# Layer norm's Newton step on VectorE, a local branch stored as half-rows, and a new order of steps

## The chip, the core and the metric

The program runs on one core of a Trainium2 chip. The metric is the device time of one execution in microseconds (us), the median of three. A core has five engines, each with its own instruction queue, worked off in order: TensorE (PE; its weight loads are shown apart as PEld), VectorE (DVE), ScalarE (ACT), GpSimd (POOL) and SyncE (SP), which here only issues DMAs. SBUF is the working memory. PSUM is the small memory that TensorE writes its results to; VectorE and ScalarE can use it too. An engine that needs another's result waits on a semaphore, and everything behind the waiting instruction in its queue waits with it.

## The reference, cut to what matters

Two layers on x of shape (32, 128, 56, 56), all in fp32. Layer 0 (a depthwise convolution, a layer norm, and a mixture of 8 experts of which each token uses 2) is not touched. Layer 1 is:

```
xh  = cv1_w @ x + cv1_b                        # 128 channels, per pixel
l   = silu(batchnorm(depthwise_conv3x3(xh)))   # the local branch
t   = (xh - mean) / sqrt(var + 1e-05)          # over the channels of a pixel
x,z = in_proj(t); x = silu(conv1d(x)); dt, B, C = x_proj(x); dt = softplus(dt_proj(dt))
h_i = exp(dt * A_i) * h_i + dt * B_i * x       # along the 3136 pixels, 16 states i, 256 channels
g   = out_proj((sum_i C_i * h_i + D * x) * silu(z))
out = x + cv2_w @ concat(l, g) + cv2_b
```

## The kernel before

Layer 1 (`layer1`, from L960) works through 224 groups, seven of 448 pixels in each of the 32 images. The 256 inner channels lie as two halves on 128 partitions, so most tiles are 128 x 896. A group has 16 units, one per state i (the recurrence of `h_i`). Each unit is a chain over the engines:

- `bc_load` (SP, L1320): a row of B (`bb`) or C (`cb`) for two states, broadcast to 128 partitions by one DMA, three buffers each
- `db_pool` (POOL, L1326): db = du * bb
- `exp_act` (ACT, L1339): da = exp(dt * A_i), two instructions, into a PSUM tile; `das` holds two such tiles, used by even and odd units in turn. A tile is 1024 columns wide, of which columns 63 to 960 are used
- `scan_dve` (DVE, L1357 and L1361): the recurrence over the 448 pixels. `MODE` gives each state a letter: in mode D the result overwrites da, in modes P and Q it goes to a tile `hs` in SBUF, in Q as two halves
- `cmul` (L1377): prod = h * cb, on VectorE for D, on GpSimd for P and Q; six buffers `prod`
- `carry_act` (ACT, L1383 and L1385): the last column of h into db, for the next group
- `sum_pe` (PE, L1286): adds the product into the PSUM tile `py`

Beside the units each group has the steps of `PLAN`: `fetch` (DMAs of x and of layer 0's result), `moe_pe`/`moe_act`, `cv1_pe` (xh, and again with centred weights for the variance), `sq_act`, `var_pe` (L1065: the variance of 4 x 112 pixels as a 112 x 4 tile), `rstd_act` and `rstd_dve` (1/sqrt of it), `bc_pe` (that, broadcast to all partitions), `te_dve` (the normalized input, L1106), `z_pe` and `xm_pe` (in_proj with the 1-D convolution folded in), the silus, `px_pe`/`px_act` (dt, B, C, and out to DRAM), `dt_pe` with `sp_abs`, `sp_exp`, `sp_one`, `sp_w`, `sp_ln`, `sp_pe`, `sp_act` (softplus), `du_pool` (L1241), `lt_pe`, `lt_act`, `lt_silu` (the local branch), and at the end `yz_dve`, `out_pe`, `out_act`. All TensorE results but `py` and the two `da` share two PSUM buffers (`mm_tile`).

The order is written out. Every entry of `PLAN` and `UNITS` has a key in units; at the end of `layer1` all steps of all groups are sorted by 16 x group + key (units: 16 x group + i + key) and emitted so. Each engine's queue is that list cut to its own steps. The steps of a group thus run from about three groups ahead of its units to two behind, and a key that changes moves the step in its engine's queue.

`rstd_act` and `rstd_dve` compute r = 1/sqrt(var + eps) as exp(-0.5 * ln(.)), refined by one Newton step, all on ScalarE: `v` = -0.5 * (var + eps) (L1072), Ln (L1074), Exp (L1075), Square (L1083), then, column by column with per-partition scales, four instructions for w * v + 1.5 (L1089) and four for the last product (L1091). `lt_act` turns the two PSUM tiles of the local branch, each holding a half of the rows on each partition half, into one tile of 128 channels x 448 pixels with four instructions of 64 partitions (L1267). `out_pe` then sums four things into `p_out`: x by the identity (L1302), the local branch by `cvlt` (L1303), and two halves of the state branch (L1306). In fp32 each matmul is recorded as two passes.

Of the kernel before, what the change touches and what calls it, by code (L numbers as in the profile page):

```python
# [13 lines left out]
C = 128  # L14
# [31 lines left out]
    (-49.034, "fetch"),  # L46
    (-34.491, "moe_pe"),
    (-33.235, "moe_act"),
    (-30.254, "cv1_pe", "p_cvc", "cv1c"),
    (-25.768, "sq_act"),  # L50
    (-25.59, "cv1_pe", "p_cv1", "cv1t"),
    (-25.289, "var_pe"),
    (-25.26, "cv1_act"),
    (-23.34, "rstd_act"),
    (-21.787, "rstd_dve", 0),
    (-21.347, "edges_act"),
    (-20.085, "rstd_dve", 1),
    (-19.667, "rstd_dve", 2),
    (-19.068, "bc_pe"),
    (-18.585, "te_dve"),  # L60
    (-17.079, "z_pe", 0),
    (-16.851, "z_copy", 0),
    (-16.382, "te_act"),
    (-16.257, "z_pe", 1),
    (-15.595, "xm_pe", 0),
    (-15.307, "xm_pe", 1),
    (-15.128, "z_copy", 1),
    (-14.156, "xm_act", 0),
    (-14.083, "z_silu"),
    (-13.778, "xm_act", 1),  # L70
    (-13.661, "px_pe"),
    (-13.36, "tables"),
    (-11.232, "px_act"),
    (-10.854, "dt_pe", 0),
    (-9.505, "dt_pe", 1),
    (-9.422, "sp_abs", 0),
    (-8.888, "sp_abs", 1),
    (-8.888, "sp_exp"),
    (-7.793, "sp_one"),
    (-6.852, "sp_w"),  # L80
    (-5.494, "sp_pe", ("w", "e", "m")),
    (-5.47, "sp_ln"),
    (-5.277, "sp_pe", ("u",)),
    (-4.8, "sp_act", 0),
    (-4.714, "sp_act", 1),
    (-4.647, "du_pool"),
    (-4.258, "lt_pe", range(0, 9)),
    (-3.101, "lt_act", 0),
    (-3.069, "lt_act", 1),
    (1.649, "lt_silu"),  # L90
    (2.601, "dd_pe"),
    (18.368, "yz_dve", 0),
    (18.991, "yz_dve", 1),
    (22.686, "out_pe"),
    (25.881, "out_act"),
# [3 lines left out]
        (-5.616, "bc_load", "cb"),  # L99
        (-4.911, "bc_load", "bb"),  # L100
        (-1.39, "exp_act"),
        (-1.071, "db_pool"),
        (-0.072, "scan_dve"),
        (0.16, "cmul", 0),
        (1.101, "carry_act"),
        (3.822, "sum_pe"),
    ),
    (
        (-2.061, "db_pool"),
        (-0.79, "exp_act"),  # L110
        (0.509, "scan_dve"),
        (1.024, "cmul", 0),
        (1.612, "carry_act"),
        (9.256, "sum_pe"),
    ),
    (
        (-6.765, "bc_load", "bb"),
        (-2.879, "db_pool"),
        (-0.932, "bc_load", "cb"),
        (-0.582, "exp_act"),  # L120
        (0.048, "scan_dve"),
        (0.16, "cmul", 0),
        (0.522, "carry_act"),
        (5.894, "sum_pe"),
    ),
    (
        (-3.304, "db_pool"),
        (-1.398, "exp_act"),
        (-0.808, "scan_dve"),
        (0.16, "cmul", 0),  # L130
        (0.573, "carry_act"),
        (1.195, "sum_pe"),
    ),
    (
        (-8.644, "bc_load", "bb"),
        (-3.115, "db_pool"),
        (-1.883, "bc_load", "cb"),
        (-1.034, "exp_act"),
        (0.401, "scan_dve"),
        (1.06, "cmul", 0),  # L140
        (1.952, "carry_act"),
        (2.601, "sum_pe"),
    ),
    (
        (-4.077, "db_pool"),
        (-0.798, "exp_act"),
        (-0.026, "scan_dve"),
        (0.16, "cmul", 0),
        (1.627, "carry_act"),
        (4.902, "sum_pe"),  # L150
    ),
    (
        (-4.927, "bc_load", "bb"),
        (-4.793, "db_pool"),
        (-2.544, "bc_load", "cb"),
        (0.282, "exp_act"),
        (0.775, "scan_dve"),
        (0.822, "cmul", 0),
        (2.269, "carry_act"),
        (2.348, "sum_pe"),  # L160
    ),
    (
        (-4.809, "db_pool"),
        (-0.316, "exp_act"),
        (-0.083, "scan_dve"),
        (1.06, "cmul", 0),
        (4.835, "sum_pe"),
        (7.392, "carry_act"),
    ),
    (  # L170
        (-5.33, "bc_load", "bb"),
        (-4.423, "db_pool"),
        (-4.3, "bc_load", "cb"),
        (-1.21, "exp_act"),
        (-0.684, "scan_dve"),
        (0.16, "cmul", 0),
        (0.81, "carry_act"),
        (0.846, "sum_pe"),
    ),
    (  # L180
        (-4.428, "db_pool"),
        (-0.91, "exp_act"),
        (-0.218, "scan_dve"),
        (0.16, "cmul", 0),
        (0.687, "carry_act"),
        (2.437, "sum_pe"),
    ),
    (
        (-6.827, "bc_load", "bb"),
        (-5.444, "bc_load", "cb"),  # L190
        (-4.717, "db_pool"),
        (-1.047, "exp_act"),
        (-0.085, "scan_dve"),
        (0.16, "cmul", 0),
        (0.563, "carry_act"),
        (1.1, "sum_pe"),
    ),
    (
        (-5.564, "db_pool"),
        (-0.852, "exp_act"),  # L200
        (0.057, "scan_dve"),
        (0.16, "cmul", 0),
        (0.848, "sum_pe"),
        (1.13, "carry_act"),
    ),
    (
        (-8.236, "bc_load", "bb"),
        (-5.146, "db_pool"),
        (-4.78, "bc_load", "cb"),
        (-0.969, "exp_act"),  # L210
        (0.064, "scan_dve"),
        (1.06, "cmul", 0),
        (3.979, "sum_pe"),
        (4.341, "carry_act"),
    ),
    (
        (-5.525, "db_pool"),
        (-0.5, "exp_act"),
        (-0.221, "scan_dve"),
        (0.16, "cmul", 0),  # L220
        (0.243, "carry_act"),
        (0.9, "sum_pe"),
    ),
    (
        (-12.437, "bc_load", "bb"),
        (-3.699, "db_pool"),
        (-2.866, "bc_load", "cb"),
        (-1.274, "exp_act"),
        (-0.7, "scan_dve"),
        (-0.009, "carry_act"),  # L230
        (0.16, "cmul", 0),
        (0.341, "sum_pe"),
    ),
    (
        (-4.484, "db_pool"),
        (-1.264, "exp_act"),
        (-0.768, "scan_dve"),
        (1.211, "cmul", 0),
        (2.733, "sum_pe"),
        (5.051, "carry_act"),  # L240
# [4 lines left out]
def tile_kernel(tc: tile.TileContext, a: dict, out: bass.AP):  # L245
# [14 lines left out]
    with (  # L260
# [414 lines left out]
        def weights(wp, wt, pw):  # L675
# [24 lines left out]
            cvlt = load(a["cv2_wT"][:C, :], [C, C], "cvlt")  # L700
# [259 lines left out]
def layer1(s):  # L960
# [12 lines left out]
    with (  # L973
# [12 lines left out]
        das = [pda.tile([128, 1024], F32, name=f"da{i}")[:, 512 - W1 : 512 + W1] for i in range(2)]  # L986
# [7 lines left out]
        one5 = one.tile([128, 1], F32, name="one5")  # L994
        nc.vector.memset(one5, 1.5)
        eps5h = one.tile([128, 1], F32, name="eps5h")
        nc.vector.memset(eps5h, -0.5e-5)
# [71 lines left out]
        def rstd_act(g):  # L1069
            d = st[g]  # L1070
            d["v"] = two.tile([TT, TPC1], F32, name="v")
            nc.scalar.activation(d["v"], d.pop("p_var")[:TT, :TPC1], AF.Identity, bias=eps5h[:TT], scale=-0.5)  # L1072
            d["r"] = two.tile([TT, TPC1], F32, name="r")
            nc.scalar.activation(d["r"], d["v"], AF.Ln, scale=-2.0)  # L1074
            nc.scalar.activation(d["r"], d["r"], AF.Exp, scale=-0.5)  # L1075

        def rstd_dve(g, k):

            d = st[g]
            r, v = d["r"], d["v"]  # L1080
            if k == 0:
                d["rw"] = two.tile([TT, TPC1], F32, name="rw")
                nc.scalar.activation(d["rw"], r, AF.Square)  # L1083
            else:
                w = d["rw"]
                for j in range(TPC1):
                    c = slice(j, j + 1)
                    if k == 1:
                        nc.scalar.activation(w[:, c], w[:, c], AF.Identity, bias=one5[:TT], scale=v[:, c])  # L1089
                    else:  # L1090
                        nc.scalar.activation(r[:, c], w[:, c], AF.Copy, scale=r[:, c])  # L1091
# [89 lines left out]
        def px_act(g):  # L1181
            d = st[g]
            xd = d["xd"] = two.tile([XR, CH1], F32, name="xd")
            nc.scalar.copy(xd, d.pop("p_x")[:XR, :CH1])
            bc_d = d["bc_d"] = s["dram2"].tile([XR, CH1], F32, name="bc_d")
            nc.sync.dma_start(out=bc_d[DR:, :], in_=xd[DR:, :])
# [72 lines left out]
        def lt_act(g, r):  # L1259
            d = st[g]  # L1260
            if r == 0:
                d["lt"] = two.tile([C, CH1], F32, name="lt")
            lt, p = d["lt"], d["p_l"][r]
            rs = slice(r * HD, (r + 1) * HD)
            for k in range(2):
                ks = slice(k * HD, (k + 1) * HD)
                nc.scalar.activation(  # L1267
                    lt[rs, k * CH1 // 2 : (k + 1) * CH1 // 2], p[ks, : CH1 // 2], AF.Identity,
                    bias=s["bnt"][ks, r, 0:1], scale=s["bnt"][ks, r, 1:2],
                )  # L1270
# [28 lines left out]
        def out_pe(g):  # L1299
            d = st[g]  # L1300
            d["p_out"] = p = mm_tile("p_out")
            nc.tensor.matmul(p[:, :CH1], lhsT=ident, rhs=d.pop("x1"), start=True, stop=False)  # L1302
            nc.tensor.matmul(p[:, :CH1], lhsT=s["cvlt"], rhs=d.pop("lt"), start=False, stop=False)  # L1303
            yz = d.pop("yz")
            for r in range(2):
                nc.tensor.matmul(p[:, :CH1], lhsT=s["wo"][:, r, :], rhs=yz[:, r, :], start=False, stop=r == 1)  # L1306

        def out_act(g):
            n, q = divmod(g, NQ1)
            ot = two.tile([C, CH1], F32, name="ot")  # L1310
# [131 lines left out]
```

## Time and profile before

| | |
|---|---|
| median of three executions | 16079.44 us (16073.9 to 16081.61) |
| the profiled execution | 16086.15 us |
| its span, first to last instruction | 16084.4 us |
| first and last `te` (L1106), 224 in all | 5914.4 and 15980.9 us |
| L1339 ACT exp, 7168 of 128 x 449 | 637 ns each |
| L1267 ACT lt, 896 of 64 x 224 | 516 to 535 ns each |
| L1089 and L1091 ACT, 896 each of 112 x 1 | 0.382 and 0.292 us each, overlapping |
| L1072, L1074, L1075 ACT, 112 x 4 | 262, 206 and 206 ns |

The page is one execution as the hardware profiler took it. Times in it are us from the span's start unless marked ns. A line of a timeline has start, duration (of merged instructions together), engine, line, operation, output<-inputs, shapes, number; in brackets the idle time of the engine just before and what ended it. A line of the waits has who waited at which line for whom, total us, times, longest. "PEclk" is the clock that TensorE was granted, as a share of full speed. "Idle" of VectorE between neighbours can be below zero: instructions of one engine overlap by some 0.08 us.

### The profile page before, as it was taken

How to read it: one execution, taken by the hardware profiler on the slowest of the kernel's cores; microseconds unless marked ns; L12 is line 12 of the kernel's file. 1: busy time of each engine (PE TensorE's matmuls, PEld its weight loads, DVE VectorE, ACT ScalarE, POOL GpSimd, SP SyncE). 2: the span in 40 equal slices, each digit the busy share in tenths (PEclk: the TensorE clock that was granted, in tenths of full speed). 3: DMA queues.
4: the chain of work that ended last, by engine and by line, in shares of the span. 5: the costliest groups of instructions: out<-in, count | busy, mean ns of one | idle time of the engine just before them, and what ended most of it. 6: DMA issues, size and time to landing. Idle time of an engine off the chain costs nothing. (4 is left out here: it accounts for less than half of the span.)

```text
span 16084.4 us, 247325 instructions
## 1 busy us (share of the span) xinstructions
PE 13000.1 (81%) x91637; PEld 7138.1 (44%) x91637; DVE 11071.4 (69%) x10582; ACT 11045.9 (69%) x23222; POOL 13580.1 (84%) x8121
## 2 busy tenths in 40 slices
PE   7996100001999989999999999999999999999998
PEld 6996100000777754444444444444444444444443
DVE  2655400000111139999999999999999999999999
ACT  4655200000444459999999999999999999999998
POOL 2443477777888879999999999999999999999999
PEclk9997555555999999999999999999999999999999
DMA  8785433332555545555555555555555555555555
GB/s 265 228 238 185 176 94 93 97 93 68 71 72 71 70 84 178 182 182 181 178 182 181 179 179 179 179 182 181 179 180 181 180 179 179 178 181 182 180 179 166
DMA packets 1239131, 2572.16 MB, mean 160 GB/s; under 512 B 139336, under 2 KB 676640, under 8 KB 1230240
## 3 DMA queue, kind: packets, MB, share of 16 engines
q1 hardware_dynamic: 1041440, 2361.89, 46.6%
q0 software_dynamic: 196480, 194.45, 7.0%
q8 instruction: 721, 11.81, 0.3%
q14 instruction: 490, 4.01, 0.1%
HBM read 2180.38 MB, written 375.43 MB: 159 GB/s over the span
## 5 line engine op out<-in xcount | busy, mean ns | idle before, releaser
L1326 POOL TENSOR_TENSOR db<-du,bb 128x896 f32<-128x896 f32 x3584 | 6835.8, 1936 | 24.8 <-DMA bb<-bc_d 21.8
L1339 ACT ACTIVATE da<-dt,aneg 128x449 f32<-128x449 f32 x7168 | 4534.9, 637 | 454.4 <-DVE prod L1377 297.4
L1357 DVE TENSOR_TENSOR_SCAN da<-da,db 128x898 f32<-128x898 f32 x2240 | 4525.4, 2020 | 157.9 <-ACT da L1339 157.2
L1286 PE MATMUL py<-prod,ident 64*64 64x448 f32 x28672 | 3279.1, 562 | 158.5 <-DVE prod L1377 150.9
L1377 POOL TENSOR_TENSOR prod<-hs,cb 128x896 f32<-128x896 f32 x1344 | 2603.9, 1937 | 153.8 <-issue 104.7
L1377 DVE TENSOR_TENSOR prod<-da,cb 128x896 f32<-128x896 f32 x2240 | 2439.3, 1089 | 233.2 <-PE py L1286 67.2
L944 ACT COPY xc<-ept 128x512 f32<-128x512 f32 (+1 forms) x248 | 143.9, 580 | 2916.5 <-PE ept L942 2614.5
L850 POOL DMA_INDIRECT buf_d<-xg,slot x1568 | 1641.9, 1047 | 538.4 <-issue 528.5
L902 POOL DMA_INDIRECT res_d<-ys,xb x984 | 1593.9, 1620 | 350.2 <-issue 287.3
L942 PE MATMUL ept<-ident,xb 128*128 128x128 f32 (+1 forms) x984 | 189.0, 274 | 2027.0 <-DMA xb<-buf_d 2023.2
L1286 PEld LDWEIGHTS py<-prod,ident 64*64 64x64 f32 x28672 | 1041.8, 134 | 1687.3 <-issue 969.6
L1357 DVE TENSOR_TENSOR_SCAN hs<-da,db 128x898 f32<-128x898 f32 x896 | 1785.6, 2014 | 0.1
L1122 PE MATMUL p_xm<-te,wk 128*128 128x448 f32 x3584 | 1416.0, 546 | 0.0
L894 DVE TENSOR_TENSOR ys<-py,b2t 128x512 f32<-128x512 f32 (+2 forms) x256 | 170.8, 670 | 1712.2 <-PE py L888 1541.6
L847 DVE COPY xg<-gate 128x28 f32<-128x28 f32 x56 | 12.7, 232 | 1896.2 <-DMA buf_d<-xg,slot 1896.2
L942 PEld LDWEIGHTS ept<-ident,xb 128*128 128x128 f32 (+1 forms) x984 | 124.6, 143 | 2030.7 <-issue 2026.3
L888 PEld LDWEIGHTS py<-w2t,hh 128*128 128x128 f32 x7872 | 938.8, 192 | 187.2 <-issue 113.1
L888 PE MATMUL py<-w2t,hh 128*128 128x128 f32 x7872 | 988.0, 279 | 11.0 <-ACT hh L884 10.7
L1122 PEld LDWEIGHTS p_xm<-te,wk 128*128 128x128 f32 x3584 | 657.5, 189 | 731.7 <-issue 567.3
L379 PE MATMUL pc<-xc,toep 112*112 112x112 f32 (+1 forms) x8192 | 937.4, 270 | 40.5 <-ACT toep L368 37.1
L1361 DVE TENSOR_TENSOR_SCAN hs<-da,db 128x449 f32<-128x449 f32 x896 | 924.9, 1074 | 1.3 <-ACT da L1339 0.9
L379 PEld LDWEIGHTS pc<-xc,toep 112*112 112x112 f32 x8192 | 880.7, 184 | 50.8 <-ACT toep L368 45.1
(238 smaller groups left out, 20802.2 us busy)
## 6 DMA issues: line engine op xcount, KB each, us to landing
cb<-bc_d SPq DMA_DIRECT2D x1792, 448.0 KB
bb<-bc_d SPq DMA_DIRECT2D x1792, 448.0 KB
toep<-toep_d SPq DMA_DIRECT2D x448, 392.0 KB
xg<-res_d SPq DMA_DIRECT2D x56, 1792.0 KB
buf_d<-zero SPq DMA_DIRECT2D x28, 2275.0 KB
xb<-buf_d SPq DMA_DIRECT2D x240, 260.0 KB
xt<-in_x SPq DMA_DIRECT2D x32, 1568.0 KB
res_d<-xa SPq DMA_DIRECT2D x128, 392.0 KB
```

The lines of the kernel that those rows point to most:

```text
L379: nc.tensor.matmul(pc[:, c, :, lo:hi], lhsT=tp[c // 2][:, c % 2, 6 - 2 * o : 8 - 2 * o, :], rhs=s4[:, c, :, lo + o - 1 : hi + o - 1], star ...
L850: apart(nc.gpsimd.indirect_dma_start(out=buf_d[:, :], out_offset=bass.IndirectOffsetOnAxis(ap=slots[k][:, o + j : o + j + 1], axis=0), in_ ...
L888: nc.tensor.matmul(py[:n, j, :], lhsT=hh[:, k, j * 128 : j * 128 + n], rhs=w2t[:, k, :], start=k == 0, stop=k == KF - 1,)
L902: apart(nc.gpsimd.indirect_dma_start(out=res_d[:, :], out_offset=bass.IndirectOffsetOnAxis(ap=xb[:n, j, C + 1 : C + 2].bitcast(I32), axis= ...
L942: nc.tensor.transpose(pt[:, j * 128 : j * 128 + n], xb[:n, j, :C], ident[:n, :n])
L1122: nc.tensor.matmul(p[:, :CH1], lhsT=s["wk"][:, k, hs], rhs=d["te"][:, k : k + CH1], start=k == 0, stop=k == DC - 1 and not first,)
L1286: nc.tensor.matmul(ps[r][h * HD : (h + 1) * HD, :CH1], lhsT=lhsT(rs, h), rhs=rhs[rs, h, :], start=start, stop=stop,)
L1326: nc.gpsimd.tensor_tensor(dbv[i][:, :, 1:], st[g]["du"], units[u].pop("bb"), ALU.mult)
L1339: e = nc.scalar.activation(da[:, h * W1 : (h + 1) * W1], st[g]["dt"][:, h, :], AF.Exp, scale=s["aneg"][:, h, i : i + 1])
L1357: nc.vector.tensor_tensor_scan(hs, da, dbs[i], 0.0, ALU.mult, ALU.add)
L1361: half(u, h, nc.vector.tensor_tensor_scan(hs2[h][:, hh], da[:, hh], dbs[i][:, hh], 0.0, ALU.mult, ALU.add))
L1377: eng.tensor_tensor(w["prod"], w["hs"][0][:, :, 1:], w["cb"], ALU.mult)
```

## The change

1. **Newton step.** `rstd_act` now issues four ScalarE instructions: Ln of the variance, var + eps, and the Exp twice, once into SBUF (`r0`) and once into four unused columns of the first `da` tile in PSUM (`aside`). `rstd_dve` is three VectorE instructions on 112 x 4 elements, each with `aside` as one operand.
2. **Local branch.** `lt` is kept as it lies in PSUM, 128 partitions x 2 x 224: two half-rows per channel. `lt_act` is two instructions of 128 partitions. `cvlt` becomes four 128 x 128 weights, each with zeros for the partitions that belong to the other half of the rows, and `out_pe` uses four matmuls of 224 columns for what was one of 448.
3. **Buffers.** `xd` and `ot` have one buffer instead of two; two constant columns go.
4. **Places.** All keys of `PLAN` and `UNITS` are new. The queues keep most of their order. VectorE's differs only by the three new steps, after the scan of state 11 (two of them) and after the scan of state 12 (one). On ScalarE `lt_silu` comes after the other silus instead of first, `edges_act` stands before the exp of state 10 instead of before that of 12, `lt_act`'s two instructions stand apart, and some carries move. On TensorE `px_pe` comes ahead of `cv1_pe` (`p_cvc`), the two `xm_pe` ahead of the sum of state 12; `sum_pe(3)` lies between the two `dt_pe`; `sum_pe(2)` moves ahead of `out_pe` and `var_pe`; the sums after `var_pe` are those of states 5, 8, 6, 1, 9 instead of 2, 6, 8, 5, 1. On GpSimd the db of state 7 moves ahead of the product of state 1 and that of 11 behind the product of 6. On SP `fetch` comes about half as far ahead, and some loads change places.

The diff, with the keys cut to those of the steps named:

```diff
-    (-25.289, "var_pe"),
-    (-23.34, "rstd_act"),
-    (-21.787, "rstd_dve", 0),
-    (-21.347, "edges_act"),
-    (-20.085, "rstd_dve", 1),
-    (-19.667, "rstd_dve", 2),
+    (-23.306, "var_pe"),
+    (-23.291, "rstd_act"),
+    (-23.185, "edges_act"),
+    (-20.935, "rstd_dve", 0),
+    (-20.876, "rstd_dve", 1),
+    (-19.458, "rstd_dve", 2),
...
-            cvlt = load(a["cv2_wT"][:C, :], [C, C], "cvlt")
+            cvlt = wp.tile([128, 2, 2, C], F32, name="cvlt")
+            nc.gpsimd.memset(cvlt, 0.0)
+            for k in range(2):
+                nc.sync.dma_start(
+                    out=cvlt[k * HD : (k + 1) * HD, k], in_=a["cv2_wT"][:C, :].rearrange("(r d) c -> d r c", r=2)
+                )
...
-        das = [pda.tile([128, 1024], F32, name=f"da{i}")[:, 512 - W1 : 512 + W1] for i in range(2)]
+        das = [pda.tile([128, 1024], F32, name=f"da{i}") for i in range(2)]
+        aside = das[0][:TT, :TPC1]
+        das = [t[:, 512 - W1 : 512 + W1] for t in das]
...
         def rstd_act(g):
             d = st[g]
-            d["v"] = two.tile([TT, TPC1], F32, name="v")
-            nc.scalar.activation(d["v"], d.pop("p_var")[:TT, :TPC1], AF.Identity, bias=eps5h[:TT], scale=-0.5)
-            d["r"] = two.tile([TT, TPC1], F32, name="r")
-            nc.scalar.activation(d["r"], d["v"], AF.Ln, scale=-2.0)
-            nc.scalar.activation(d["r"], d["r"], AF.Exp, scale=-0.5)
+            p = d.pop("p_var")[:TT, :TPC1]
+            rl, d["v"], d["r0"] = (two.tile([TT, TPC1], F32, name=n) for n in ("rl", "v", "r0"))
+            nc.scalar.activation(rl, p, AF.Ln, bias=eps5[:TT])
+            nc.scalar.activation(d["v"], p, AF.Identity, bias=eps5[:TT])
+            nc.scalar.activation(aside, rl, AF.Exp, scale=-0.5)
+            nc.scalar.activation(d["r0"], rl, AF.Exp, scale=-0.5)
 
         def rstd_dve(g, k):
 
             d = st[g]
-            r, v = d["r"], d["v"]
             if k == 0:
-                d["rw"] = two.tile([TT, TPC1], F32, name="rw")
-                nc.scalar.activation(d["rw"], r, AF.Square)
+                nc.vector.scalar_tensor_tensor(aside, aside, -0.5, d["r0"], ALU.mult, ALU.mult)
+            elif k == 1:
+                nc.vector.tensor_tensor(aside, aside, d.pop("v"), ALU.mult)
             else:
-                w = d["rw"]
-                for j in range(TPC1):
-                    c = slice(j, j + 1)
-                    if k == 1:
-                        nc.scalar.activation(w[:, c], w[:, c], AF.Identity, bias=one5[:TT], scale=v[:, c])
-                    else:
-                        nc.scalar.activation(r[:, c], w[:, c], AF.Copy, scale=r[:, c])
+                d["r"] = two.tile([TT, TPC1], F32, name="r")
+                nc.vector.scalar_tensor_tensor(d["r"], aside, 1.5, d.pop("r0"), ALU.add, ALU.mult)
...
-                d["lt"] = two.tile([C, CH1], F32, name="lt")
-            lt, p = d["lt"], d["p_l"][r]
-            rs = slice(r * HD, (r + 1) * HD)
-            for k in range(2):
-                ks = slice(k * HD, (k + 1) * HD)
-                nc.scalar.activation(
-                    lt[rs, k * CH1 // 2 : (k + 1) * CH1 // 2], p[ks, : CH1 // 2], AF.Identity,
-                    bias=s["bnt"][ks, r, 0:1], scale=s["bnt"][ks, r, 1:2],
-                )
+                d["lt"] = two.tile([128, 2, CH1 // 2], F32, name="lt")
+            nc.scalar.activation(
+                d["lt"][:, r, :], d["p_l"][r][:, : CH1 // 2], AF.Identity,
+                bias=s["bnt"][:, r, 0:1], scale=s["bnt"][:, r, 1:2],
+            )
...
             nc.tensor.matmul(p[:, :CH1], lhsT=ident, rhs=d.pop("x1"), start=True, stop=False)
-            nc.tensor.matmul(p[:, :CH1], lhsT=s["cvlt"], rhs=d.pop("lt"), start=False, stop=False)
+            lt = d.pop("lt")
+            for k in range(2):
+                for r in range(2):
+                    nc.tensor.matmul(
+                        p[:, k * CH1 // 2 : (k + 1) * CH1 // 2], lhsT=s["cvlt"][:, k, r, :], rhs=lt[:, r, :],
+                        start=False, stop=False,
+                    )
```

## Prediction

> **What bounds the kernel now.** I read the page's busy shares first. No engine stands alone over the whole run:
>
> ```profile
> PE 13000.1 (81%) x91637; PEld 7138.1 (44%) x91637; DVE 11071.4 (69%) x10582; ACT 11045.9 (69%) x23222; POOL 13580.1 (84%) x8121
> ```
>
> The change touches only layer 1, from about 5900 us on, so next the busy time by stretch (columns: PE, PEld, DVE, ACT, POOL busy, then granted clock, DMA share, GB/s):
>
> ```profile
> 8000.00:9000.00 1000.00, 953.21 (x6757) 434.06 (x6757) 961.61 (x687) 914.73 (x1986) 965.24 (x517) 0.96 0.56 181
> ```
>
> Four engines are 91 to 97% busy; ACT, the engine that the change relieves, is the least busy. What counts is where VectorE waits, since its scans carry the recurrence and every loop of waits runs through it. The waits of VectorE, over the span:
>
> ```profile
> DVE da L1357 <- ACT da L1339: 157.2, 273, 1.0
> DVE prod L1377 <- PE py L1286: 67.2, 56, 1.2
> ```
>
> 273 waits for an exp, 56 for TensorE. The timelines put each at one place. From `te` (L1106) to `te` 222 groups take 45.19 us on average. 168 without a VectorE stall on TensorE take mostly 44.86; 54 take 46.3. In the common kind VectorE stands at one scan, that of state 13:
>
> ```profile
> 8921.76 2.02 DVE L1357 TENSOR_TENSOR_SCAN hs<-da,db 128x898 f32<-128x898 f32 x1
> 8924.47 2.04 DVE L1357 TENSOR_TENSOR_SCAN da<-da,db 128x898 f32<-128x898 f32 x1 [0.69 <-ACT da L1339]
> ```
>
> ScalarE at that moment:
>
> ```profile
> 8919.07 1.31 ACT L1339 ACTIVATE da<-dt,aneg 128x449 f32<-128x449 f32 x2
> 8920.33 0.95 ACT L1236 COPY dt<-p_sp 128x448 f32<-128x448 f32 x2
> 8921.17 1.22 ACT L1089 ACTIVATE rw<-rw,one,v 112x1 f32<-112x1 f32 x4
> 8922.29 0.15 ACT L1385 COPY db<-da 128x2 f32<-128x2 f32 x1
> 8922.33 0.86 ACT L1091 ACTIVATE r<-rw,r 112x1 f32<-112x1 f32 x4
> 8923.08 2.53 ACT L1339 ACTIVATE da<-dt,aneg 128x449 f32<-128x449 f32 x4
> ```
>
> The reader is to see that the Newton step (L1089, L1091) stands in ScalarE's queue between the exps of states 12 and 13, and that the scan's 0.69 us is its lateness.
>
> The 46.3 us groups are another matter. Their granted clock:
>
> ```profile
> 10080.00:10081.00 1.00, 0.29 (x1) 1.00 1.03 416
> 10081.00:10082.00 1.00, 1.00 (x6) 0.69 0.92 355
> 10082.00:10083.00 1.00, 1.00 (x8) 0.50 0.74 272
> ...
> 10087.00:10088.00 1.00, 1.00 (x2) 0.50 0.00 0
> 10088.00:10089.00 1.00, 1.00 (x5) 0.90 0.00 0
> ```
>
> TensorE runs at half clock for 6.8 us, just after the thin `p_dt` matmuls (8 rows) and a wait for ScalarE. In half-us stretches the half-clock spells last 3.41 or 6.83 us, in 186 of the 222 groups: 132 short, 54 long. They begin 20.6 to 22.9 us after `te`, at multiples of 3.413 us. I work with a rule read off these phases: a 3.41 us window with less than about 1.47 us of full-height matmul work makes the next one half-speed. A short spell loses 1.7 us of TensorE and stalls nobody; a long one loses 3.4 and stalls VectorE 1.46.
>
> **The change, part by part.** The sum is for the profiled run (span 16084.4, with 1.75 us around it 16086.15), which is 6.7 above the median of 16079.44; the difference is then put on the median.
>
> *The Newton step leaves ScalarE.* Gone from between the exps of 12 and 13: 1.22 + 0.86 us, and the Square (0.19) ahead. The scan of state 13 then waits for nothing known: exp 12 starts when the product of state 10 is done, and exp 13 needs the product of 11, finished 1.9 us before scan 12 is; an exp pair takes 1.25. I take the whole 157 us; at worst, where something else is late there, none.
>
> *It arrives on VectorE* as three 112x4 instructions after scan 11 and scan 12. Nearest rows:
>
> ```profile
> L403 DVE SCALAR_TENSOR_TENSOR nm<-mv,rs 112x7 f32<-112x7 f32 x128 | 120.6, 951 | 2.0
> L584 DVE SCALAR_TENSOR_TENSOR cand<-step,cand 128x4 f32<-128x4 f32 x48 | 7.8, 162 | 5.1 <-ACT sign L552 0.5
> ...
> L583 DVE TENSOR_SCALAR step<-p_tot 128x4 f32<-128x4 f32 x48 | 7.5, 157 | 0.5 <-PE p_tot L568 0.5
> ```
>
> L403 reads two SBUF operands while GpSimd computes: 143 to 2050 ns. With GpSimd idle (L584) 162, with a PSUM operand (L583) 157. The new ones have one operand in PSUM and run beside GpSimd, like `prod<-da,cb`, which takes 1074 to 1094 ns there throughout. So 0.157 each. VectorE's neighbours overlap by 0.08 when independent and gap 0.11 when one needs the other; the three fill the gap between scan 11 and its product and open one between themselves: 3 x 0.157 - 0.25 = 0.22 us a group, 49 us in 224. Bounds: 0, and 3 x (0.157 + 0.11) = 0.80 us, 179.
>
> *Waits added.* The operand shares PSUM tile da[0] with the even exps, so the accesses must be ordered. ScalarE writes it after product 8, which exp 10 waits for anyway; behind it stand `edges` and exp 10. The first VectorE step must follow exp 12 (over 0.4 us before scan 11 ends); behind it stands product 11. Exp 14 must follow the third, which ends 0.08 us after scan 12; behind exp 14 stands `lt_act`, and scan 14 needs it 3 us later. I take 0; the worst, 0.4 a group. The Trainium skill, "PSUM — Partial Sum Buffer", section "PSUM bank collisions raise a hardware error", speaks against the placing: two engines in one bank and quadrant at the same time are an error, whatever the columns. No run here shows a collision; by that rule the order above is a must, and the sum is the same while those margins hold.
>
> *`lt_act`*: four of 529 ns (L1267) become two, -1.06 us of ScalarE, in a place where ScalarE waits 1.26 us for VectorE next: 0. The four `rstd_act` instructions stand for three, 0.2 us each: 0.
>
> *The padded weights.* The `lt` part of `p_out` (L1303) takes 0.75 us unthrottled (8908.37 to 8909.12: two passes of 0.375). It becomes eight passes of 224 columns. Half of 0.375 is 0.19; the 112-column passes of `p_bc` take 0.14, the 448-column ones 0.375. I take 0.2: 1.6, +0.85 us a group (0.4 to 2.25). TensorE has 2 us idle a group; what decides is the place. `var_pe` comes after `p_out`, and ScalarE's queue holds `rstd_act` ahead of exp 10, which scan 10 needs. In the unthrottled group at 8884.7, `var` is done at 8911.41, ScalarE wants it at 8912.64, and exp 10 is 0.69 early: 1.9 us of margin, which covers one half-clock window (1.7) and lacks 1.5 for two: the 1.46 seen. The change eats the margin: +0.85 from the passes, +0.8 from `sum_pe(2)` put ahead of `p_out`, -0.3 for a wait that goes, +0.2 for `edges` put ahead of exp 10, -0.3 because `px` is early. Left: 0.4 to 0.9. A short spell would now stall 0.8 to 1.3, a long one 2.5 to 3.0.
>
> *How often?* `sum_pe(3)` moves between the two `p_dt`, and the second `p_dt` takes a buffer freed by `sq` instead of `sp_abs`, so its 0.93 wait shrinks to about 0.1, while a wait of 0.7 opens ahead of the first. By my rule starts between 19.6 and 21.1 us after `te` are caught, 1.45 of 3.41 us of phase, long ones only up to 20.05. The phase moves with (group time - 13 x 3.413 = 44.37). At 44.86 it drifted 0.49 a group and was caught nearly always. The new group is 44.86 - 0.69 + 0.22 = 44.39 to 44.6: it drifts 0 to 0.2, and a stall of 1 us throws it out of the caught range. Between two short stalls in 33 groups (1.7 us) and two short and a long one in 12 (4.2 us) that is 0.05 to 0.35 us a group; I take 0.25, 56 us, where 54 x 1.46 = 79 us stand now: -23.
>
> The Trainium skill, "TensorE: Matmul & The Clock Gate", section "Why this matters for your kernels", asks only for no TensorE idle gap over about 3 us; here the longest wait in that stretch is 1.0 and the clock falls all the same, so the rows decide. By the page the spells would not exist, and the sum without their term would be -107.
>
> *Else.* GpSimd keeps its order but for single swaps and has 1.3 us of slack at `du` and product 12. On SP the bb and cb loads keep 5 us or more ahead of use; `x1` is fetched 19 us ahead; single `xd` and `ot` buffers are free 40 us before reuse. The new weight load is a few DMAs and a memset among the 1568 scatters: under 1 us. The last `p_out` adds 1.
>
> Sum: -157 + 49 - 23 + 1 = -130 us: 15956 by the profiled run, **15950** on the median.
>
> **Rivals.** *The clock takes it back (slower).* If the caught range is wider or the walk off by 0.3 us, a stalled group lands in the range again, and nearly each group pays. It decides from (108 + 79) / 222 = 0.84 us of stall a group. At 1.5: 333 - 187 = +146, 16225; spread 16100 (one group in two, at 1.9) to 16425 (each, at 2.4). For: 186 of 222 groups are caught now, and `var` comes later. Against: the small drift.
>
> *Nothing comes of it.* Exp 10, or another step just in time, is late by what scan 13 no longer waits, 0.5 us: 16079, between 16047 and 16111. For: four engines over 91%. Against: ScalarE stands idle 3 us a group, so it can catch up.
>
> *GpSimd blocks the small steps.* If the PSUM operand did not spare them L403's 951 ns, 3 x 0.8 us x 224 = +537: 16490. Against: every `prod` row.
>
> **How the numbers follow.** Forecast 0.57, nothing 0.15, clock 0.25, blocking 0.03. The forecast's own range is 15890 to 16040; the range 15890 to 16170 leaves out the worse half of the clock rival, the blocking and a little below. Faster by over 0.2% (32 us, about what can be told from no change) 0.57, within 0.15, slower 0.28.
>
> **What would show it.** Right: no [<-ACT da] at scan 13, three 0.16 us steps on VectorE, groups of 44.4 to 44.6, L1303's eight passes in 1.6 us, half-clock spells in fewer than half the groups. Wrong: ScalarE's `Ln` waiting on `p_var` by over 0.5 us in most groups with scan 10 late behind it; small steps over 0.3 us; exp 14 or the first step waiting for the other engine.

## The result, and the profile after

The changed kernel takes 16,164.59 us (median of 5; 16,157.39 to 16,168.8), the kernel before 16,081.16 beside it: ratio **1.0052**, 95% interval 1.0038 to 1.0067. It is slower by 83 us. The forecast was 15,950; the time lies in the range, on the other side of no change.

The profiled execution has a span of 16,167.1 us. From `te` to `te` (now L1105) 222 groups take 45.61 us on average, where it was 45.19: 93 us in all, of which 10 come back because layer 1 starts that much earlier. The waits of VectorE over the span (who waited at which line for whom; total us, times, longest):

```profile
DVE da L1358 <- ACT da L1340: 241.8, 207, 2.5
DVE prod L1378 <- DMA cb<-bc_d: 65.4, 92, 2.0
```

The waits for exp have grown from 157.2 to 241.8 us, those for TensorE's `py` (67.2 us before) are down to one of 3.2, and a wait for the cb loads is new. Yet the scan that stood late before is not late any more. VectorE from the scan of state 11 to that of 13:

```profile
8603.47 2.03 DVE L1358 TENSOR_TENSOR_SCAN da<-da,db 128x898 f32<-128x898 f32 x1
8605.41 0.14 DVE L1085 SCALAR_TENSOR_TENSOR da<-da,r 112x4 f32<-112x4 f32 x1
8605.58 0.17 DVE L1087 TENSOR_TENSOR da<-da,v 112x4 f32<-112x4 f32 x1
8605.66 1.08 DVE L1378 TENSOR_TENSOR prod<-da,cb 128x896 f32<-128x896 f32 x1
8606.66 2.02 DVE L1358 TENSOR_TENSOR_SCAN hs<-da,db 128x898 f32<-128x898 f32 x1
8608.59 0.14 DVE L1090 SCALAR_TENSOR_TENSOR r<-da,r 112x4 f32<-112x4 f32 x1
8608.65 2.03 DVE L1358 TENSOR_TENSOR_SCAN da<-da,db 128x898 f32<-128x898 f32 x1
```

The three small steps stand where they were put, and no idle time is left between them and scan 13. A group with no stall takes 44.0 to 44.3 us, mostly 44.13; it took 44.86. So each usual group gained 0.73 us, about 162 us in all, and more than that was lost elsewhere. The next group (`te` at 8613.71) shows where. Its granted clock (after the busy times come clock, DMA share, GB/s):

```profile
8633.00:8634.00 1.00, 1.00 (x10) 0.29 (x2) 0.96 (x2) 1.00 (x3) 1.00 (x2) 1.00 0.30 118
8634.00:8635.00 1.00, 1.00 (x3) 0.43 (x2) 1.00 (x2) 0.84 (x4) 1.00 (x1) 0.72 0.52 108
8635.00:8636.00 1.00, 1.00 (x2) 0.00 (x0) 1.00 (x1) 0.97 (x2) 1.00 (x2) 0.50 1.02 319
8636.00:8637.00 1.00, 1.00 (x9) 0.44 (x12) 1.00 (x2) 0.84 (x3) 1.00 (x1) 0.50 1.07 240
8637.00:8638.00 1.00, 1.00 (x12) 0.36 (x8) 1.00 (x1) 0.97 (x3) 1.00 (x2) 0.57 0.97 233
8638.00:8639.00 1.00, 1.00 (x9) 0.30 (x2) 1.00 (x2) 1.00 (x4) 1.00 (x2) 1.00 1.00 394
```

and the timeline that follows, all engines, cut to the chain:

```profile
8639.45 1.68 PE L1301 MATMUL p_out<-lt,cvlt 128*128 128x224 f32 x8
...
8642.46 0.85 PE L1068 MATMUL p_var<-mean_w,sq 128*112 128x1 f32 x8
...
8643.36 0.26 ACT L1076 ACTIVATE rl<-p_var,eps 112x4 f32<-112x4 f32 x1 [1.17 <-PE p_var L1068]
...
8644.13 1.31 ACT L1340 ACTIVATE da<-dt,aneg 128x449 f32<-128x449 f32 x2
...
8645.54 2.04 DVE L1358 TENSOR_TENSOR_SCAN da<-da,db 128x898 f32<-128x898 f32 x1 [0.97 <-ACT da L1340]
```

One half-clock window of 3.4 us makes `p_out` and `var` late. ScalarE stands 1.17 us at the Ln, exp 10 is behind it, and scan 10 pays 0.97. Before, such a short spell cost nothing. 73 groups have a short spell and take mostly 45.20 us; 86 have a long one (6.83 us) and take 46.81, waiting at scan 10 for 0.7 to 2.5 us, mostly 2.0, and 62 of them also at scan 8, mostly for 0.4. The time at half clock is nearly the same as before in total (847 us in layer 1, 836 before). What has grown is the number of long spells (86, where it was 54) and what each spell costs.

The waits for cb come at two places, products 5 and 8: the loads of C's rows 4 and 8 are issued late on SP.

### The profile page after: what moved, and what is told of

It reads as the page before. It is cut to its first block, busy times and chain, and to the rows that moved or that the text cites. A ratio compares the mean times of both kernels' runs of the same rounds, so it can differ in the third digit from the quotient of the medians.

```text
span 16167.1 us, 249143 instructions
## 1 busy us (share of the span) xinstructions
PE 13186.2 (82%) x92981; PEld 7186.3 (44%) x92981; DVE 11127.7 (69%) x11252; ACT 10394.7 (64%) x20982; POOL 13570.6 (84%) x8122
## 5 line engine op out<-in xcount | busy, mean ns | idle before, releaser
L1358 DVE TENSOR_TENSOR_SCAN da<-da,db 128x898 f32<-128x898 f32 x2240 | 4526.1, 2021 | 243.7 <-ACT da L1340 241.8
L1281 PE MATMUL py<-prod,ident 64*64 64x448 f32 x28672 | 3421.3, 578 | 121.5 <-DVE prod L1378 96.0
L1253 PE MATMUL p_l<-xh,dwd 64*64 64x224 f32 x16128 | 907.5, 352 | 7.7 <-ACT dt L1235 2.2
```

The lines of the kernel that those rows point to most:

```text
L1253: nc.tensor.matmul(d["p_l"][r][k * HD : (k + 1) * HD, : CH1 // 2], lhsT=s["dwd"][rs, t, rs], rhs=d["xh"][rs, dy + k * R : dy + (k + 1) * R ...
L1281: nc.tensor.matmul(ps[r][h * HD : (h + 1) * HD, :CH1], lhsT=lhsT(rs, h), rhs=rhs[rs, h, :], start=start, stop=stop,)
L1358: nc.vector.tensor_tensor_scan(hs, da, dbs[i], 0.0, ALU.mult, ALU.add)
```

## Experiments

**The theories.** *Clock*: half-clock spells of TensorE make `var` late, the new order and the longer `p_out` have used up the margin, and scan 10 pays. *Loads*: the late cb loads are what costs. *Small steps*: the three VectorE steps, or their ordering with the even exps through the shared PSUM tile, cost what they save. *Weights* and *places* are the two sides of the clock theory: which part of the change took the margin.

Three sets of four kernels ran beside the kernel before, which took 15,887 us in the first, 16,087 in the second and 15,881 in the third set. The 200 us lie ahead of layer 1 (the first `te` of the runs comes at 5,705 to 5,718 us in the first and third set and at 5,913 to 5,918 in the second). So ratios to the kernel before of the same set are compared, and the mean group of the profiled execution. The times expected for the first set reckon with 16,081 for the kernel before, those for the second with 15,887; they are read as differences to it. Spells are those of the 222 groups, by the granted clock.

| run | ratio (95% interval) | mean group | spells 3.4 / 6.8 / 10.2 us |
|---|---|---|---|
| before | 1 | 45.19 | 132 / 54 / 1 |
| changed | 1.0052 (1.0038 to 1.0067) | 45.61 | 73 / 86 / 0 |
| e1_var_early | 1.0028 (1.0016 to 1.0039) | 45.46 | 84 / 23 / 51 |
| e2_loads | 1.0037 (1.0025 to 1.0049) | 45.58 | 91 / 87 / 0 |
| e3_fill | 0.9945 (0.9932 to 0.9959) | 44.87 | 37 / 22 / 0 |
| e4_newton | 0.9885 (0.987 to 0.99) | 44.37 | 134 / 24 / 1 |
| e5_newton_weights | 0.9957 (0.9943 to 0.997) | 44.88 | 139 / 34 / 0 |
| e6_old_lt | 0.9964 (0.9951 to 0.9978) | 44.98 | 113 / 51 / 0 |
| e7_sum2_back | 0.9949 (0.9935 to 0.9962) | 44.82 | 85 / 43 / 0 |
| e8_newton_fill | 0.9862 (0.9846 to 0.9877) | 44.20 | 3 / 0 / 0 |
| e9_mended | 0.9889 (0.9874 to 0.9904) | 44.37 | 73 / 8 / 0 |
| e10_all_fill | 0.9863 (0.9848 to 0.9878) | 44.21 | 4 / 0 / 0 |
| e11_before_fill | 0.9952 (0.9938 to 0.9965) | 44.82 | 1 / 0 / 0 |
| e12_thin_fill | 0.9887 (0.9871 to 0.9902) | 44.36 | 125 / 22 / 0 |

### e1_var_early: the variance ahead of p_out

```diff
-    (-23.306, "var_pe"),
+    (-24.7, "var_pe"),
```

> The changed kernel with one key altered: `var_pe` is issued ahead of `out_pe` instead of behind it, so the variance no longer stands behind the longer `p_out`. Clock theory (half-clock spells make `p_var` late, ScalarE's Ln and the exp of state 10 behind it wait, and scan 10 pays): VectorE's waits for exp, 242 us in the changed kernel, fall under 60, and so the time falls by about 200 us to 15,920 to 15,980, while the spells themselves stay; ScalarE's waits for `p_var` fall below 30 us. Loads theory (late cb loads are what costs): at most some 20 us change, 16,145 to 16,185, the 65 us of waits for cb stay. Small-steps theory (the Newton steps' ordering with the exps costs): no change.

A miss: 56 us over the kernel before, where 101 to 161 under it were expected. The waits for exp did fall from 241.8 to 53.0 us, but the time hardly did. VectorE's waits:

```profile
DVE prod L1378 <- DMA cb<-bc_d: 81.3, 121, 2.1
DVE da L1358 <- issue: 73.8, 75, 1.5
DVE da L1358 <- ACT da L1340: 53.0, 73, 1.3
DVE prod L1378 <- PE py L1281: 34.5, 41, 1.0
```

The 75 waits with no releaser named are at scan 13. On ScalarE the exps of 13 and 14 come behind the copies of `p_sp`, and `p_sp` stands behind `p_out` on TensorE:

```profile
7909.53 0.97 ACT L1235 COPY dt<-p_sp 128x448 f32<-128x448 f32 x2 [1.93 <-PE p_sp L1281]
...
7910.69 2.54 ACT L1340 ACTIVATE da<-dt,aneg 128x449 f32<-128x449 f32 x4
```

With scan 10 on time, this later wait shows. And the spells grew: 51 last 10.24 us now, where there was none. These 51 groups take 47.74 us each and hold 184 of the 295 us that the 222 groups of e1 lie above 44.13. `var`'s matmuls (one column each) had moved into the spell, which I take for the cause without a run that shows it. So a late TensorE is paid at the next place that waits for it; moving one consumer does not end it.

### e2_loads: the loads in their old places

The keys of `bc_load` are those of the kernel before, for example:

```diff
-        (-4.093, "bc_load", "bb"),
+        (-8.644, "bc_load", "bb"),
...
-        (-0.666, "bc_load", "cb"),
+        (-1.883, "bc_load", "cb"),
```

> The changed kernel with the keys of `bc_load` (bb and cb) as they were before the change, the rest left. Loads theory: the 65 us of waits for cb on VectorE go and the time falls by at least as much, 16,100 or less. Clock theory: the waits for cb go too, but they had also thrown groups out of the phase in which the half clock catches them, so part is paid back in waits for exp: 16,100 to 16,165, with more than 242 us of waits for exp.

```profile
DVE da L1358 <- ACT da L1340: 290.1, 260, 2.4
```

The waits for cb are gone altogether, and 48 of their 65 us are back as waits for exp: 178 groups are caught instead of 159. The mean group fell by 0.03 us. The clock theory had it so; the loads are no cause of their own while the clock catches the groups.

### e3_fill: work for TensorE where it waited

```diff
+        def fill_pe(g):
+            d = st[g]
+            if g:
+                tiles(py(g - 1), lambda rs, h: wzero[rs, :], d["xm"], False, False)
...
+    (-11.25, "fill_pe"),
     (-11.215, "dt_pe", 0),
```

`wzero` is a tile of zeros: the eight passes, on the four quarters of the array, add 0 to `py`.

> The changed kernel with 8 matmul passes of zero weights added into `py` ahead of the first `p_dt` of each group (the sum is the same), where TensorE waited about 1.2 us for ScalarE. Clock theory with the rule of the prediction (a window with too little matmul work halves the clock of the next): the half-clock spells become rare, under 50 of 222 groups, VectorE's waits for exp fall below 60 us, and the time is 15,900 to 15,980 though TensorE has 0.9 us more to do in each group. If 64-row matmuls do not count as work for the clock, the spells stay at over 150 groups and the time is 16,150 to 16,300. Loads theory: 16,150 or more in either case, from the work added.

59 spells are left instead of 159, the waits for exp are 75.1 us instead of 241.8, and 0.74 us a group is gained although TensorE does about 1 us more. The direction is the clock theory's, the size falls short: 78 us under the kernel before, where 101 to 181 were expected; 59 spells (under 50) are left, and the cb waits have grown to 87.3 us.

### e4_newton: the Newton step alone

The kernel before with the new `rstd_act`, `rstd_dve` and `aside`, and only these keys changed:

```diff
-    (-21.787, "rstd_dve", 0),
-    (-20.085, "rstd_dve", 1),
-    (-19.667, "rstd_dve", 2),
+    (-20.94, "rstd_dve", 0),
+    (-20.88, "rstd_dve", 1),
+    (-19.458, "rstd_dve", 2),
```

> The kernel before with the Newton step alone moved to VectorE (the same four ScalarE and three VectorE instructions with the operand in PSUM, the two first steps between scan 11 and product 11, the third behind scan 12); all other keys, the local branch and its weights as before. If the Newton part does what the prediction said and only the new places and weights spoil it: no wait for exp at scan 13, groups of 44.1 to 44.3 us without a stall, a long spell now and then with a stall of about 1.5, 15,890 to 15,960. If the small steps or their ordering with the even exps cost what they save: 16,050 to 16,150.

15,703.83 beside 15,886.84: 183 us less, where 121 to 191 were expected. Most groups take 44.18 us, and what VectorE waits for TensorE is small:

```profile
DVE prod L1375 <- PE py L1284: 33.4, 45, 1.2
```

The small-steps theory is out. The exp of state 14 does wait for the third step, 112.9 us in all (0.5 a group), and no scan is late for it.

### e5_newton_weights and e6_old_lt: the weights, added and taken away

e5 is e4 with the change's `lt_act`, `cvlt` and `out_pe`, in the old places (and one buffer for `xd` and `ot`). e6 is the changed kernel with these three as they were.

> The run with the Newton step alone on VectorE in the old places (15,704 beside 15,887 for the kernel before) plus the half-row local branch with padded weights (and one buffer for `xd` and `ot`), still in the old places. Weights theory (the 0.75 to 0.85 us that p_out's lt part takes longer is what makes `var` late): most of the loss is here, 15,800 to 15,920, with waits for exp on VectorE over 60 us. Places theory (the new keys make `var` late and bring the half clock to a worse phase; the weights alone only use up margin): 15,700 to 15,760 and hardly any wait for exp.

> The changed kernel with the old local branch (`lt` as 128 x 448, four `lt_act`, one matmul in `p_out`), new places and Newton step kept. The changed kernel would be about 15,969 beside this run's 15,887 if its ratio of 1.0052 holds. Weights theory: `var` comes 0.75 us earlier, the stalls of both kinds of half-clock groups shrink by 0.75: about 120 us less, 15,830 to 15,870. Places theory: less than half of it, 15,910 to 15,970.

In the old places the weights cost 0.50 us a group (44.37 to 44.88), as the weights theory had it (74 us under the kernel before; 87 under to 33 over), but not by the wait that it named: VectorE's waits for exp are 0.9 us in all, where over 60 were expected. Scan 10 stays on time; the products wait for their buffers, which the sums on TensorE free:

```profile
DVE prod L1382 <- PE py L1285: 137.2, 175, 2.6
```

In the new places taking them away gains 0.63 (45.61 to 44.98), 59 us under the kernel before where 17 to 57 were expected, and the waits for exp fall from 241.8 to 71.1 us. So the weights theory was right on the size; the wait that pays depends on the places.

### e7_sum2_back: one sum behind the variance again

```diff
-        (3.828, "sum_pe"),
+        (6.7, "sum_pe"),
```

> The changed kernel with `sum_pe(2)` behind `var_pe` again. If TensorE's order is what holds `p_out` and `var` in the half-clock groups, they come 0.8 us earlier and the stalls shrink as much: 15,830 to 15,880. If `p_out` waits there for its PSUM buffer (`sp_abs(1)` on ScalarE reads it last), nothing is gained: 15,930 to 15,980.

0.80 us a group (45.61 to 44.82), more than the weights alone and more than expected (84 us under the kernel before; 7 to 57), and the waits for exp fall to 28.7 us: TensorE's order holds `p_out`, not its buffer. The gains of e6 and e7 add to 1.43 us, where all waits for exp were 242 / 222 = 1.09: each alone brings the short spells nearly back under the margin (groups with a short spell take 44.46 and 44.42 us instead of 45.20), and long spells become fewer (51 and 43 instead of 86) and cheaper (46.06 us in both, instead of 46.81). It is a threshold, not a sum of prices.

### e8_newton_fill and e12_thin_fill: what the clock counts

Both are e4 with a filler ahead of the second `p_dt` (and one buffer for `ot`). In e8 it is e3's, which fills both 64-row halves of the array. In e12 it has 8 rows:

```diff
+                for r in range(1):
+                    for h in range(2):
+                        nc.tensor.matmul(
+                            py(g - 1)[r][h * HD : (h + 1) * HD, :CH1], lhsT=wzero[:DR, :], rhs=d["xm"][:DR, h, :],
+                            start=False, stop=False,
+                        )
```

> The run with the Newton step alone in the old places plus the filler of zero weights (8 passes added into `py`) ahead of the second `p_dt`, where TensorE waits 0.5 to 0.9 us (and one buffer for `ot`). Clock theory: fewer half-clock spells than the 159 of the run without it, and no long ones, groups 44.2 us throughout: 15,660 to 15,690. If the spells only move or the filler itself makes later work late: 15,700 to 15,760.

> The Newton step alone in the old places, with a filler in the same place ahead of the second `p_dt`, but of 8 rows: two matmuls (four passes) of zero weights of 8 x 64, added into `py`. If what the clock counts is only that TensorE is busy, the spells go as with the filler of 64 rows: fewer than 20, groups of 44.18. If matmuls of few rows don't count as work, the spells stay as in the run without a filler: 130 to 200 groups, 44.25 to 44.45 us on average.

The two fillers as groups (count, busy us, mean ns), first e8's, then e12's:

```profile
L1287 PE MATMUL py<-xm,wzero 64*64 64x448 f32 x1784 | 219.1, 562 | 0.0
```

```profile
L1305 PE MATMUL py<-xm,wzero 8*64 8x448 f32 x892 | 217.3, 563 | 0.0
```

They keep TensorE busy for the same time, and both end its wait for `sp_m` there (193.2 us in e4, 0.3 in each). The clock from 7000 to 15000 us, e8 and then e12:

```profile
7000.00:15000.00 8000.00, 7829.64 (x56935) 3512.97 (x56930) 7873.52 (x6155) 7174.54 (x14790) 7888.29 (x4215) 1.00 0.57 184
```

```profile
7000.00:15000.00 8000.00, 7841.38 (x55950) 3503.72 (x55946) 7846.73 (x6128) 7145.61 (x14736) 7851.88 (x4199) 0.97 0.57 183
```

With all rows at work the half clock is gone (3 spells) and the groups take 44.18 throughout. With 8 rows nothing changes against e4 (147 spells, 44.36). So it isn't TensorE's idle time that lets the clock fall here, but how much of the array works. The fillers differ in the number of passes as well (eight and four a group), but passes don't decide either. All changes of the clock lie on one grid of 3.41 us. Cut on this grid, layer 1 of e12 has 146 windows at full clock that are followed by half clock: they hold at most 1.60 us of matmuls with 64 rows or more, though up to 15 passes, and in 126 of them TensorE is busy for over 3.0 us. The 2563 that are followed by full clock hold at least 1.52 us of such matmuls, some with only 9 passes. In the kernel before the two limits are 1.57 and 1.54 us. In e12, in a group that begins at 7071.5, the clock is halved from 7092 on, though TensorE has paused for only 0.33 us in the 6 us before:

```profile
7090.27 1.02 PE L1036 MATMUL p_cv<-x,cv1t 128*128 128x448 f32 x2
7091.22 1.02 PE L1305 MATMUL py<-xm,wzero 8*64 8x448 f32 x4
7092.22 1.86 PE L1192 MATMUL p_dt<-xd,dtt 8*128 8x448 f32 x2
```

The `p_dt` that follows takes 1.86 us instead of 1.01.

### e9_mended, e10_all_fill, e11_before_fill: putting it together

e9 is the changed kernel with e3's filler, e7's key and e2's loads; e10 is e5 with e8's filler; e11 is the kernel before with e8's filler.

> The changed kernel, all its parts kept, with three mends: the filler of zero weights ahead of the first `p_dt`, `sum_pe(2)` behind `var_pe`, and the bb and cb loads in the places of the kernel before. Clock theory: the unstalled group of the changed kernel, 44.0 to 44.15 us, becomes the usual one, under 60 half-clock spells are left and cost 0.2 (short) to 1.5 us each, no waits for cb: groups of 44.1 to 44.3 us on average, 0.83 to 1.0 under the 45.14 of the kernel before, ratio 0.986 to 0.989. If the new order is worse than the old by something other than the clock and the loads: groups over 44.5, ratio above 0.991.

> The run with Newton step and padded weights in the old places (groups of 44.83 us, 110 us over the one with the Newton step alone) plus the filler ahead of the second `p_dt`. Clock theory: the longer p_out costs only through the half clock, so without spells the weights cost nothing: groups of 44.15 to 44.25 us, ratio to the kernel before 0.985 to 0.988, fewer than 20 spells. If the extra 0.8 us of TensorE costs by itself (products waiting for the sums): groups of 44.5 to 44.8, ratio 0.991 to 0.996.

> The kernel before plus the filler alone (and one buffer for `ot`). Clock theory: the long spells' stalls of 1.46 us in 54 groups go, the wait at scan 13 for the Newton step stays: groups of 44.8 to 44.9 us, 60 to 80 us less, ratio 0.995 to 0.9965, fewer than 20 spells. If the clock was no loss in the kernel before, or the filler costs as much as it saves: ratio 0.998 to 1.002.

All three came out as the clock theory had it, but for e9's 81 spells (under 60 expected) and its 44.37 us (44.1 to 44.3). Its groups without a spell take 44.13 and those with a short one 44.40. e10 says most: with the clock held up, the padded weights and the single buffers cost nothing (44.21 beside e8's 44.20), and the whole change but its places takes 0.9863 (0.9848 to 0.9878) of the kernel before. e11 shows what the spells cost before: 0.37 us a group, 77 us by the medians. e8 and e10 are the fastest kernels here, level with each other; e9, with the new places, stays 0.16 us a group behind e10.

## Why the prediction was wrong, step by step

- **The Newton step off ScalarE: right in kind, too low in size.** The usual group of e4 is 0.68 us shorter. The sum took 0.69 for the wait less 0.22 for the new steps, 0.47.
- **Three steps on VectorE: right in kind, too high in size.** They take 145, 170 and 135 ns (0.157 taken). From the start of scan 11 to that of 13 it was 5.85 us with the wait and is 5.17 in e4; without wait and steps the rows give 5.07 (2.13 from scan to product, 1.01 on to scan 12, 1.93 on to scan 13). So the steps cost 0.10 us a group, not 0.22, and the wait 0.78: the 0.69 and an overlap of some 0.08 that a wait takes away.
- **Waits through the shared tile: right.** Exp 14 waits 0.5 us a group for the third step and costs nothing. The rule of the Trainium skill's page "PSUM — Partial Sum Buffer", section "PSUM bank collisions raise a hardware error", that spoke against the placing is not tested by this: the accesses are ordered, and no run shows two engines in the bank at once.
- **Padded weights: right.** Eight passes, 1.66 to 1.68 us (1.6 taken). The size of the margin as well: a short spell was to stall 0.8 to 1.3 and stalls 0.97; a long one 2.5 to 3.0, and its groups are 2.68 longer than the unstalled ones. But the prediction laid the old 1.46 us of a long spell to exp 10 alone. In the group whose clock it shows, product 9 waits first, for its buffer, which the sums on TensorE free:

```profile
10090.81 1.09 DVE L1377 TENSOR_TENSOR prod<-da,cb 128x896 f32<-128x896 f32 x1 [1.23 <-PE py L1286]
...
10092.10 2.04 DVE L1357 TENSOR_TENSOR_SCAN da<-da,db 128x898 f32<-128x898 f32 x1 [0.20 <-ACT da L1339]
```

Exp 10 ends at 10091.99, so it was late by about as much as the two waits together, and the size came out right. In the old places it is the product's wait that grows with the weights (e5), in the new ones scan 10's.

- **"How often?": this step failed.** It said that the group "drifts 0 to 0.2, and a stall of 1 us throws it out of the caught range", 0.25 us a group. Spells hit 159 of 222 groups, and the stalls for exp come to 1.09 us a group. The range is wider: but for single ones, starts lie between 18.7 and 21.2 us after `te`, where 19.6 to 21.1 was read off, and long spells start up to 20.4 in groups that wait for nothing else (20.05 taken). Worse, the sum priced a stall without following it into the next group. In 3.413 us windows, a group of 46.81 us is 14 windows less 0.97, so the next one meets the window border 0.97 later; one of 45.20 is 13 windows plus 0.83, so 0.83 earlier. A long spell that starts at 19.9 is followed by a short one at 20.9, that by a long one at 20.05, and so on. The stall does not free the group, it locks it in: pairs of 92.01 us against 27 windows of 92.16. The trace bears it out: of the 73 short spells 60 are followed by a long one in the next group, of the 86 long ones 56 by a short one. No run tests the locking alone; e2 speaks for it, since without the cb waits, which throw groups out of step, 178 groups are caught instead of 159. This is the rival "the clock takes it back", which had a chance of 0.25; its condition (the range wider) and its side were right. That the time lies inside the stated range is owed to the better half of this rival, which the range took in, and not to the forecast.
- **"Else": wrong on the loads.** "5 us or more ahead of use" failed for two loads of cb, 65 us; e2 shows that most of these are no loss of their own.
- **The rule against the page: shown.** The Trainium skill, "TensorE: Matmul & The Clock Gate", section "What's actually happening", has a free-running window of 3413 ns and a clock set by how busy TensorE has been. The spells here last 3.41 us or a multiple, which agrees. That TensorE's busy time decides does not: e8's and e12's fillers keep it busy for 219.1 and 217.3 us in the same place, and the runs have 3 and 147 spells. The prediction's own rule, about 1.47 us of full-height matmul work in a window, comes out at about 1.55 (e12 and the kernel before, above).

By groups: 222 x (44.13 - 44.86) = -162 us from the usual group. Above it the changed kernel loses 222 x (45.61 - 44.13) = 329 us, of which 242 waits for exp, 65 for cb and some 20 not placed one by one; the kernel before lost 222 x (45.19 - 44.86) = 73. Together +94, beside 93 measured. (That the sum agrees follows from the means; what it tells is how the loss is shared out.) What brought the margin down, the weights or the moved sum, can't be split: either taken back alone brings most of it back.

## What to carry to other kernels

A wait that is taken away shortens the period of a loop, and everything that runs on a clock of its own is met at new phases: follow a stall into the next round before pricing how often it happens, since it can lock the loop in as well as free it. Margins have thresholds: a step of 0.8 us of slack was worth nothing while spells stayed under it and 140 to 180 us once they did not. And where half-clock spells recur, look for matmuls with few rows ahead of them; a filler that uses the whole array, in the gap before them (here 0.98 us of TensorE), was worth 77 us to the old kernel and made the padded weights free.

## What was not expected of the hardware

- TensorE can be busy nearly without a break and still have its clock halved, when many of the matmuls use 8 of 128 rows (e12, 147 groups; in 126 of its 146 windows ahead of a spell it is busy for over 3.0 of 3.41 us). Matmuls of zero weights count as work (e8).
- `var`'s matmuls of one column, moved forward to where the spells are, went with 51 spells of 10.24 us where there had been none (e1).
- Beside a working GpSimd, VectorE steps on 112 x 4 with one operand in PSUM take 133 to 171 ns in all 672 cases of the changed kernel; none was slowed.
